# Layer 1's transposes and hub loads within the mixing, and two terms of the convolution's first two pairs ahead of it

## The chip, the cores and the metric

The kernel runs on one core of one Trainium2 chip. The metric is the device time of one launch in microseconds (us). All times below come from the runs and the one profiled execution of the kernel before.

## The reference

Four graph layers act on x of shape (8, 2048, 64): 8 batches, 2048 nodes, 64 features. Each layer is `x = x + gnn(relu(layernorm(x)))`. The adjacency `adj` is 2048 x 2048, zeros and ones with a full diagonal. The first nodes (the hubs) have many neighbours and the last few.

The change lies between the end of layer 0 and the first part of layer 1. Layer 0 ends with a mixing, a softmax of two scores, `tanh(f @ fcW + fcb) @ av`, over two candidates. Layer 1 is a Chebyshev convolution with weights of its own for each node, made from a 16-wide embedding:

```python
w = einsum('nd,dkio->nkio', embedding, weight)          # k = 0, 1, 2
b = embedding @ bias
A_stack = [I, A, 2*A@A - I]
x_g = einsum('knm,bmc->bnkc', A_stack, h)               # h = relu(layernorm(x))
out = einsum('bnki,nkio->bno', x_g, w) + b
```

So it needs A h (the first product in the sense of the layer; the kernel's text and this document call the run that makes it the second product, after layer 0's own adjacency product), and A (A h), made chunk by chunk beside the convolution.

## The kernel before, in words

Data lie either "by feature", as four pairs q of two batches (128 rows of features by 2048 nodes), or "by node", as 16 tiles t of 128 nodes by 512 (8 batches of 64 features). A chunk is 512 nodes, so four tiles. Six large buffers, q0 to q5, are reused through the layers. The program is written in an order, and a planner reorders it for each engine by its own durations, inside the buffers that each tile has. Within an engine's queue the instructions then run in the planned order.

**Mixing** (`mix`, L686 to L773). It steps over four chunks and four pairs. `attend` (L711) scores the next pair ahead; then come the tanh, the mix, the store of x (L767), and the norm of the chunk (`norm_parts`, L271), whose last step, `write` (L697), puts h into `xe` and `xo` (q0 to q3). `each` (L861) brings in and transposes gathered rows. `beside` is `Lists.fill` (L2472): 60 indirect DMAs on POOL read listed blocks of the adjacency, and DVE masks them into `cells`, in bf16. The last chunk's x and its scratch lie in q4 and q5 (`end`, L693), the others' in q6 to q8.

**Passage and second product** (`layer1_near`, L1624). `lists.load` (L2506) loads the adjacency rows of the three hubs (`dense`) and the first columns of the other 13 tiles (`zero`), and DVE casts them to bf16. A loop over 16 tiles transposes h to nodes (L1647), copies it to `ah` in q4 and q5 and stores it in DRAM (`sent[0]`, L1649). Then for each target tile t `Feed.target` (L2629) adds up A h in PSUM: three hub tiles (`dense`, L2610) and LISTED[t] listed pieces (`listed`, L2616). For each piece POOL gathers 128 rows of `sent` (L2578), ACT makes the high part (L2595), DVE the low part (L2596), PE multiplies both with weights that ACT casts from `cells` (L2554) or `dense` (L2564). `finish` (L2634) puts the sum into `ah`; it is stored in `sent[1]` (L1672), and `turn` (L1653) transposes it back into the other halves of `xe` and `xo`. Target 0 has no lists: it reads the 13 tiles from `ah` itself.

**Convolution** (`convolution_near`, L1679). It loads its weights, subtracts (L1697) and doubles (L1698) them, loads the embedding of the first chunk (`load_emb`) and makes A (A h) for that chunk (`product(0)`). Then for chunks 1, 0, 2, 3 in this order, four pairs, eight blocks b and two halves it runs

```python
self.mm(pk, w01[half][:, c], src(q)[:, s], stop=False)      # L1822: terms k = 0 and 1
self.mm(pks[b, half], w2[h, c], aah[h, q], start=False)     # L1829: term k = 2
y = (pks[b, half] + bias) * emb[:, b]                       # L1834, DVE
acc = acc + y                                               # L1840, POOL; the last b on DVE
```

with the next chunk's product spread between the blocks by `advance`. Each f32 matmul shows as two PE passes in the trace.

Of the kernel before, what the change touches and what calls it, by code (L numbers as in the profile page):

```python
# [7 lines left out]
F = mybir.dt.float32  # L8
# [5 lines left out]
OP = mybir.AluOpType  # L14
# [32 lines left out]
F16 = mybir.dt.float16  # L47

# [86 lines left out]
class Kernel:  # L135
# [550 lines left out]
    def mix(self, slots, ind, g, fcw, av, each=None, beside=None):  # L686
# [17 lines left out]
        with (  # L704
# [6 lines left out]
            def attend(ch, q):  # L711
# [9 lines left out]
                if q == 0:  # L721
                    bufs[ch] = end if ch == NC - 1 else [b[:, ch % 2] for b in big]
                    nc.sync.dma_start(bufs[ch][0], self.xs[0][ch])
# [14 lines left out]
            for ch in range(NC):  # L738
                s = slice(ch * CW, (ch + 1) * CW)
                x, sq, xr = bufs[ch]  # L740
                for q in range(NP):
# [22 lines left out]
                    if q < 2:  # L764
                        next(norm, None)
                    next(beside, None)
# [3 lines left out]
            for _ in norm:  # L770
                pass
            for _ in beside:
                pass  # L773
# [8 lines left out]
    def layer0_pairs(self, slots, far):  # L782
# [8 lines left out]
        with tc.tile_pool(reuse_waits="tile", name="k0", bufs=1) as k:  # L791
# [84 lines left out]
            )  # L876
            with tc.tile_pool(reuse_waits="tile", name="filling", bufs=1) as w:
                self.mix(slots, ind, h_t, fcw, av, each, lambda bank: self.lists.fill(cells, w))
# [745 lines left out]
    def layer1_near(self, slots, k2, far):  # L1624
# [11 lines left out]
        with (  # L1636
            tc.tile_pool(reuse_waits="tile", name="cheb", bufs=2) as w,
            tc.tile_pool(reuse_waits="tile", name="cheb_ps", bufs=2, space=PSUM) as ps,
        ):
            lists.load(w)  # L1640
            hub = Hub(w, "first_hub")
            for t in range(NT):
                s = slice(t * P, (t + 1) * P)
                for i, (src, h) in enumerate(((xo, hi), (xe, lo))):
                    pt = ps.tile([P, NP, D], F, name="pt", tag=("acc", "pz")[i], bufs=3)
                    for q in range(NP):
                        nc.tensor.transpose(pt[:, q], src(q)[h, s], ident[h, h])  # L1647
                    self.copy(columns(ah(t), i), pt)
                nc.sync.dma_start(self.sent[0][s], ah(t))  # L1649
                if t < HUBS:  # L1650
                    hub.fill(self, t, ah(t))

            def turn(t):  # L1653
                s = slice(t * P, (t + 1) * P)
                pz = ps.tile([P, NP, P], F, name="pz", bufs=3)
                for q in range(NP):
                    nc.tensor.transpose(pz[:, q], ah(t)[:, q * P : (q + 1) * P], ident)
                for i in range(2):
                    qs = slice(2 * i, 2 * i + 2)
                    nc.scalar.copy(xo.tiles[i][lo, :, s], pz[lo, qs])  # L1660
                    nc.vector.tensor_copy(xe.tiles[i][hi, :, s], pz[hi, qs])

            feed = Feed(self, lists, w, self.sent[0], lambda jt: ah(jt))
            for t in range(NT):
                acc = ps.tile([P, CW], F, name="acc", bufs=3)
                feed.target(acc, t, hub)
                if t < HUBS:
                    nc.scalar.copy(ah(t), acc)
                    lists.hub.fill(self, t, ah(t))
                else:  # L1670
                    feed.finish(ah(t), ah(t), acc, t)
                nc.sync.dma_start(self.sent[1][t * P : (t + 1) * P], ah(t))  # L1672
                if t > 0:
                    turn(t - 1)
            turn(NT - 1)
        with tc.tile_pool(reuse_waits="tile", name="k1", bufs=1) as k:
            self.convolution_near(slots, k)

    def convolution_near(self, slots, k):  # L1679
# [3 lines left out]
        lo, hi = slice(0, D), slice(D, P)  # L1683

        DO = DE * D
        w01 = []
# [1443 lines left out]
```

## Time and profile before

| | us |
|---|---|
| median of 3 runs (lowest to highest) | 2026.12 (2022.63 to 2032.97) |
| profiled execution, its own time | 1975.97 |
| its span, first to last instruction | 1974.2 |
| mixing, first tanh to last mix | 486.8 to 601.7 |
| norm of the last chunk, to its last write | to 617.3 |
| first store of sent[0] issued | 620.0 |
| first indirect gather of the second product | 640.5 |
| first store of sent[1] issued, last | 645.8, 737.8 |
| first chunk's product, first gathered piece at ACT | 747.5 |
| convolution's first result on DVE | 787.5 |

Over the whole span PE was busy 86%, DVE 71%, POOL 52% and ACT 41%. Busy times are of one execution. PE's are modelled: matmuls overlap, so a busy PE is not at its peak. "PEclk" is the share of full speed that was granted to TensorE. In a group's row "128x512 f32" is partitions by elements, "xN" the number of instructions, then come the busy time and the mean of one in ns; behind the second bar is the time that the engine was idle just before these instructions, with what ended it. In a timeline's row the first number is the start, the second the duration of the merged group.

### The profile page before, as it was taken

The page shows a single profiled execution, that of the slowest core. Times are in us where ns is not written, and L with a number is a line of the kernel's source. Part 1 is how long each engine was busy: PE and PEld are TensorE (multiplying, and loading weights), DVE is VectorE, ACT ScalarE, POOL GpSimd, SP SyncE. Part 2 cuts the span into 40 slices and gives each one's busy share as a digit, 9 for nine tenths or more (in the row PEclk, how much of TensorE's full clock was granted, in tenths as well). Part 3 has the DMA queues.
Part 4 walks back from the last instruction along what each step waited for, and adds up shares of the span by engine and source line. Part 5 has one row for each costly group of instructions (what it writes and reads, how often), then busy time and mean ns, then how long its engine had stood idle before and what let it go on. Part 6 is the DMA issues. An engine that isn't in the chain of part 4 may idle for free. (4 is left out here: it accounts for less than half of the span.)

```text
span 1974.2 us, 22337 instructions
## 1 busy us (share of the span) xinstructions
PE 1699.7 (86%) x7066; PEld 971.8 (49%) x7066; DVE 1408.2 (71%) x2389; ACT 809.4 (41%) x1627; POOL 1035.1 (52%) x959
## 2 busy tenths in 40 slices
PE   6859889999997887999999999778989899579885
PEld 2515666665324454444443444356767566345432
DVE  6778778884677674877677656588989676459774
ACT  5712344454664663222111010255666664267300
POOL 1100166766870743876765635266375641478771
PEclk8868899998996888999999989889989999689887
DMA  9740223345335776233131111277788774666665
GB/s 345 263 120 1 77 75 102 109 128 178 99 101 174 239 218 188 78 87 117 47 99 53 48 67 41 96 223 234 246 257 286 222 259 164 228 186 172 183 177 195
DMA packets 124057, 305.20 MB, mean 155 GB/s; under 512 B 29312, under 2 KB 31120, under 8 KB 118160
## 3 DMA queue, kind: packets, MB, share of 16 engines
q0 software_dynamic: 45328, 149.60, 25.2%
q1 hardware_dynamic: 76288, 149.80, 22.5%
q10 hardware_dynamic: 2304, 4.20, 0.6%
q8 instruction: 59, 0.97, 0.2%
q14 instruction: 78, 0.64, 0.1%
HBM read 240.40 MB, written 63.14 MB: 154 GB/s over the span
## 5 line engine op out<-in xcount | busy, mean ns | idle before, releaser
L2578 POOL DMA_INDIRECT raw<-sent,index x300 | 313.8, 1046 | 308.3 <-DVE part_lo L2596 156.3
L2596 DVE TENSOR_TENSOR part_lo<-raw,part_hi 128x512 fp32r<-128x512 f32 x352 | 266.2, 777 | 119.3 <-ACT part_hi L2595 108.8
L2595 ACT CAST part_hi<-raw 128x512 fp32r<-128x512 f32 x352 | 212.5, 619 | 319.0 <-PE acc L176 211.6
L1840 POOL TENSOR_TENSOR half<-half,y 128x512 f32<-128x512 f32 x192 | 247.3, 1318 | 134.0 <-DVE y L1834 128.8
L176 PE MATMUL pk<-q,w 128*128 128x512 f32 (+1 forms) x768 | 301.6, 610 | 2.4 <-DVE q L1724 0.9
L176 PE MATMUL acc<-q,ident 128*128 128x512 f32 x416 | 202.3, 613 | 22.7 <-DVE q L2909 16.5
L176 PE MATMUL acc<-part_hi,weights 128*128 128x512 f32 x365 | 177.0, 488 | 27.3 <-ACT part_hi L2595 26.7
L1834 DVE SCALAR_TENSOR_TENSOR y<-pk,bias,q 128x512 f32<-128x512 f32 x224 | 158.0, 742 | 52.1 <-PE pk L176 32.9
L176 PEld LDWEIGHTS pk<-q,w 128*128 128x128 f32 (+1 forms) x768 | 115.8, 190 | 156.0 <-issue 120.2
L176 PE MATMUL acc<-part_lo,weights 128*128 128x512 f32 x365 | 167.5, 460 | 23.3 <-DVE part_lo L2596 22.7
L2819 POOL DMA_INDIRECT ring<-f_rows,near x121 | 142.8, 1180 | 64.6 <-issue 29.6
L176 PEld LDWEIGHTS acc<-q,ident 128*128 128x128 f32 x416 | 77.1, 194 | 96.4 <-issue 43.6
L2305 POOL TENSOR_TENSOR q<-q,beta 128x512 f32<-128x512 f32 x57 | 76.1, 1337 | 72.4 <-DVE beta L2281 33.8
L176 PEld LDWEIGHTS acc<-part_hi,weights 128*128 128x128 f32 x365 | 73.7, 202 | 79.4 <-ACT part_hi L2595 45.8
L176 PEld LDWEIGHTS acc<-part_lo,weights 128*128 128x128 f32 x365 | 73.9, 202 | 73.5 <-DVE part_lo L2596 57.8
L176 PE MATMUL pp<-adj,x_ind_hi 128*128 128x512 f32 x256 | 89.3, 464 | 0.5 <-DVE q L846 0.3
L2564 ACT CAST hub_weights<-dense 128x384 fp32r<-128x384 bf16 x80 | 40.6, 511 | 102.6 <-PE acc L176 98.2
L2890 DVE TENSOR_TENSOR q<-ring,e 128x1024 f32<-128x1024 f32 x58 | 70.0, 1218 | 8.7 <-PE acc L176 8.5
L2305 POOL TENSOR_TENSOR q<-q,coef 128x512 f32<-128x512 f32 x57 | 63.1, 1108 | 20.9 <-DVE q L2328 17.6
L176 PE MATMUL pp<-adj,x_ind_lo 128*128 128x512 f32 x256 | 72.7, 403 | 0.0
L287 DVE RECIPROCAL std<-std 128x512 f32<-128x512 f32 x16 | 53.6, 3351 | 25.5 <-ACT std L286 21.6
L2489 POOL DMA_INDIRECT listed_raw<-in_adjT_dram,cell x60 | 62.2, 1037 | 16.5 <-issue 15.9
(503 smaller groups left out, 3421.6 us busy)
## 6 DMA issues: line engine op xcount, KB each, us to landing
rows<-in_adj_dram SPq DMA_DIRECT2D x16, 1024.0 KB, 9.2
adj_t<-in_adjT_dram SPq DMA_DIRECT2D x64, 256.0 KB, 3.0
own<-sent SPq DMA_DIRECT2D x52, 256.0 KB, 4.3
raw<-sent SPq DMA_DIRECT2D x52, 256.0 KB, 3.5
sent<-u SPq DMA_DIRECT2D x48, 256.0 KB, 3.7
q<-x SPq DMA_DIRECT2D x10, 1024.0 KB, 5.1
x<-q SPq DMA_DIRECT2D x9, 1024.0 KB, 4.0
links<-squares POOLq DMA_DIRECT2D x16, 512.0 KB, 8.2
```

The lines of the kernel that those rows point to most:

```text
L176: self.nc.tensor.matmul(out, lhsT, rhs, start=start, stop=stop)
L287: nc.vector.reciprocal(std, std)
L1834: nc.vector.scalar_tensor_tensor(y, pks[b, half], bias[:, b : b + 1], emb[:, b], op0=OP.add, op1=OP.mult,)
L1840: add.tensor_add(acc, acc, y)
L2305: self.nc.gpsimd.tensor_tensor(x, x, by.unsqueeze(2).to_broadcast([P, NB, D]), op=OP.mult)
L2489: self.kern.behind(nc.gpsimd.indirect_dma_start(raw[:, i], None, rows, bass.IndirectOffsetOnAxis(ap=self.cell[:, c + i : c + i + 1], axis= ...
L2564: self.nc.scalar.copy(to, self.lists.dense[:, :, i * P : (i + 1) * P])
L2578: self.nc.gpsimd.indirect_dma_start(raw, None, self.rows[:], bass.IndirectOffsetOnAxis(ap=self.lists.index[:, c : c + 1], axis=0),)
L2595: nc.scalar.copy(hi, raw)
L2596: nc.vector.tensor_sub(lo, raw, hi.bitcast(F))
L2819: self.nc.gpsimd.indirect_dma_start(to, None, self.kern.f_rows[:], bass.IndirectOffsetOnAxis(ap=index, axis=0))
L2890: nc.vector.tensor_tensor(y.rearrange("n i (b f) -> n i b f", b=NB), block[:, i : i + 2, : NB * D].rearrange("n i (b f) -> n i b f", b=NB) ...
```

## The change

- *Transposes.* `mix` takes a function `turned`. It does the transposes, copies and the store in `sent[0]` for one tile. Tiles 0 to 11 are done in the last two steps of the next chunk, tiles 12 to 15 after the last norm. The last chunk's x and scratch move from q4 and q5 to the shared buffers, since `ah` now fills q4 and q5.
- *Hub loads.* `fill` also loads `dense` and `zero` in blocks of 128 x 512, and ACT casts them; `load` is gone. `cells`, `dense` and `zero` are u8 instead of bf16.
- *Two terms early.* A class `Conv` holds the convolution's weights, PSUM banks and embedding from the start of layer 1. From target 9 on, `first_part` makes for the first chunk's pairs 0 and 1 the terms k = 0 and 1 (32 matmuls), adds the bias, multiplies by the embedding and sums over b. In the convolution those pairs then have only the term k = 2; its product with the embedding is added to the sum already there, and of its 32 adds half are on DVE.
- *PSUM.* The second product now shares the convolution's banks: 6 for `pk`, which its transposes use too, and 2 for `acc` instead of 3.

```diff
@@ mix @@
                 if q == 0:
-                    bufs[ch] = end if ch == NC - 1 else [b[:, ch % 2] for b in big]
+                    last = ch == NC - 1 and turned is None
+                    bufs[ch] = end if last else [b[:, ch % 2] for b in big]
...
                     if q < 2:
                         next(norm, None)
+                    elif ch > 0 and turned is not None:
+                        for i in range(2):
+                            turned((ch - 1) * TC + 2 * (q - 2) + i, bank)
                     next(beside, None)
...
+            if turned is not None:
+                for t in range(NT - TC, NT):
+                    turned(t, bank)
@@ layer0_pairs @@
+            def turned(t, bank):
+                s = slice(t * P, (t + 1) * P)
+                for i, (src, h) in enumerate(((xo, slice(D, P)), (xe, slice(0, D)))):
+                    pt = bank()[:, : NP * D].rearrange("n (q f) -> n q f", q=NP)
+                    for q in range(NP):
+                        nc.tensor.transpose(pt[:, q], src(q)[h, s], self.ident[h, h])
+                    self.copy(columns(ah(t), i), pt)
+                nc.sync.dma_start(self.sent[0][s], ah(t))
@@ layer1_near @@
-            lists.load(w)
-            hub = Hub(w, "first_hub")
-            for t in range(NT):
...
-                    self.copy(columns(ah(t), i), pt)
-                nc.sync.dma_start(self.sent[0][s], ah(t))
+            conv = Conv(self, slots, k, ps)
+            with tc.tile_pool(reuse_waits="tile", name="cheb", bufs=2) as w:
+                hub = Hub(w, "first_hub")
+                for t in range(HUBS):
+                    hub.fill(self, t, ah(t))
...
+                    acc = ps.tile([P, CW], F, name="acc", bufs=2)
...
+                    if t == NT // 2:
+                        conv.begin()
+                    if t > NT // 2:
+                        for _ in range(2):
+                            next(conv.early, None)
+                turn(NT - 1)
+                for _ in range(8):
+                    next(conv.early)
@@ convolution_near @@
             for _ in product(0):
+                next(conv.early, None)
+            for _ in conv.early:
                 pass
...
+                    begun = place == 0 and q < conv.EARLY
...
-                                self.mm(pk, w01[half][:, c], src(q)[:, s], stop=False)
+                                if not begun:
+                                    self.mm(pk, w01[half][:, c], src(q)[:, s], stop=False)
...
-                                self.mm(pks[b, half], w2[h, c], aah[h, q], start=False)
+                                self.mm(pks[b, half], w2[h, c], aah[h, q], start=begun)
...
+                                if begun:
+                                    nc.vector.tensor_mul(y, pks[b, half], emb[:, b])
...
+                                    own = b == NBLK - 1 or begun and b % 2
+                                    add = nc.vector if own else nc.gpsimd
@@ Lists.fill @@
-        self.cells = pool.tile([P, PLACE[NT], P], BF, name="cells")
+        self.cells = pool.tile([P, PLACE[NT], P], U8, name="cells")
+        self.dense = pool.tile([P, HUBS, N], U8, name="dense")
+        self.zero = pool.tile([P, FAR, P], U8, name="zero")
...
+        def take():
+            if blocks:
+                to, src = blocks.pop(0)
+                raw = w.tile([P, CW], F, name="block_raw", bufs=3)
...
+                nc.sync.dma_start(raw, src)
+                taken.append((to, raw))
+        def store():
+            to, raw = taken.pop(0)
+            self.kern.behind(nc.scalar.copy(to, raw))
...
+            if len(taken) > 1:
+                store()
+            take()
             yield
@@ Conv.first_part @@
+        for q in range(self.EARLY):
+            for b in range(NBLK):
+                for half, src in enumerate(self.xs):
+                    pk = self.bank()
+                    self.kern.mm(pk, self.w01[half][:, b * P : (b + 1) * P], src(q)[:, s])
+                    acc = self.accs[q][half]
+                    y = self.k.tile([P, CW], F, name="early_y", bufs=2) if b else acc
+                    nc.vector.scalar_tensor_tensor(
+                        y, pk, self.bias[:, b : b + 1], self.emb[:, b], op0=OP.add, op1=OP.mult,
+                    )
+                    if b:
+                        add = nc.vector if b % 2 else nc.gpsimd
+                        add.tensor_add(acc, acc, y)
+                    yield
```

## The prediction

> **What bounds the kernel now.** I read the stretches first, busy time by engine, cut where layer 0's mixing ends and where the parts of layer 1 begin: mixing, the passage to layer 1, the second product in two halves, the first chunk's product, the convolution's first chunk.
>
> ```profile
> core 0: us, PE busy (x) PEld busy (x) DVE busy (x) ACT busy (x) POOL busy (x), PEclk, DMA share, GB/s
> 485.00:612.00 127.00, 113.95 (x396) 37.25 (x395) 80.42 (x105) 75.90 (x104) 89.07 (x85) 0.92 0.38 117
> 612.00:634.00 22.00, 13.52 (x131) 11.40 (x132) 19.48 (x34) 10.73 (x27) 0.00 (x0) 0.50 0.61 199
> 634.00:690.00 56.00, 46.62 (x153) 28.83 (x154) 35.59 (x57) 36.70 (x75) 36.49 (x36) 0.87 0.77 241
> 690.00:742.00 52.00, 42.14 (x162) 30.22 (x160) 36.55 (x63) 32.15 (x72) 26.19 (x27) 0.83 0.73 220
> 742.00:787.00 45.00, 32.30 (x96) 18.39 (x98) 18.36 (x28) 16.89 (x35) 15.78 (x15) 0.80 0.64 193
> 787.00:903.00 116.00, 113.72 (x372) 51.48 (x369) 92.67 (x108) 28.40 (x58) 88.80 (x72) 1.00 0.31 88
> ```
>
> In the passage POOL does nothing and PE runs at half clock. In both products no engine is full: they wait on chains. The convolution's first chunk is PE's (98%), with DVE at 80% behind it. Next the timelines of the passage, engine by engine (start, duration, what ended the idle time):
>
> ```profile
> 611.64 5.67 DVE L701 TENSOR_TENSOR q<-q,bank 64x512 f32<-64x512 f32 x8 [2.16 <-PE bank L176]
> ...
> 617.45 4.10 PE L1647 MATMUL pt<-ident,q 64*128 64x64 f32 x56 [2.22 <-DVE q L701]
> ...
> 631.95 1.23 DVE L2512 CAST dense<-dense_raw 128x2048 bf16<-128x2048 f32 x1 [0.88 <-DMA dense_raw<-in_adjT_dram]
> ...
> 626.23 9.61 SPq L1649 DMA_DIRECT2D sent<-q  x12
> ...
> 640.46 1.33 POOL L2578 DMA_INDIRECT raw<-sent,index  x1 [44.59 <-DMA sent<-q]
> ```
>
> All transposes wait for the last write of the norm (617.3). The first gather needs all sixteen stores of sent, the last issued at 635.8; it starts 4.6 us later. The third hub load holds PE's first product matmul until 633.8. Last, the groups by shape, from the second product (634 to 742) and then from the convolution's first chunk (787 to 903):
>
> ```profile
> L2596 DVE TENSOR_TENSOR part_lo<-raw,part_hi 128x512 fp32r<-128x512 f32 x60 | 40.4, 692 | 16.7 <-ACT part_hi L2595 14.1 <-ACT hub_weights L2564 1.8
> L2595 ACT CAST part_hi<-raw 128x512 fp32r<-128x512 f32 x60 | 36.8, 619 | 28.6 <-DMA raw<-sent,index 23.8 <-PE acc L176 2.8 <-DVE part_lo L2596 1.7
> ...
> L1840 POOL TENSOR_TENSOR half<-half,y 128x512 f32<-128x512 f32 x48 | 64.2, 1368 | 18.4 <-DVE y L1834 18.2
> L1834 DVE SCALAR_TENSOR_TENSOR y<-pk,bias,q 128x512 f32<-128x512 f32 x56 | 39.2, 740 | 7.9 <-POOL half L1840 4.3 <-PE pk L176 3.3
> L2596 DVE TENSOR_TENSOR part_lo<-raw,part_hi 128x512 fp32r<-128x512 f32 x31 | 38.1, 1249 | 9.6 <-ACT part_hi L2595 9.4
> ```
>
> The second product waits for gathers (ACT 23.8 us for DMA) and hands the wait on to DVE and PE. The same subtraction takes 0.69 us there and 1.25 us where POOL adds beside it. DVE's own eight adds in the first chunk took 9.72 us, 1.2 each.
>
> **What the Trainium skill says.** "SBUF — State Buffer", section "Who interferes with whom": a DVE instruction with two SBUF inputs contends with a GpSimd one that reads SBUF, through one shared read interface. The trace agrees: 692 against 1249 ns. "TensorE: Matmul & The Clock Gate", section "What's actually happening": the clock is gated to half after an idle window of about 3.4 us. It agrees: after 604.7 to 609.5 without matmuls the clock is 0.50, and passes start 0.43 us apart instead of 0.23. "ScalarE: Activation LUTs", section "What ACT_TABLE_LOAD costs": one element per cycle and lane, fp32 and bf16 alike. Here 512 f32 took 0.62 us and 384 bf16 0.51; no run shows u8.
>
> **The change part by part** (us; minus is saved).
>
> *Mixing.* Twelve tiles' transposes come in: 96 at 0.073 (56 in 4.10) is 7 of PE; 24 copies, half on ACT at 0.38, half on DVE at 0.42, are 4.5 and 5. The hub blocks are 16 ACT casts to u8; by the nearest row (0.62) 9.9. ACT goes from 76 to 90 of 127, DVE from 80 to 85. SP gets 16 loads and 12 stores, 0.33 each or 9, between its x loads and stores; the DMA share was 0.38, and 7 MB in 127 us add 55 GB/s to 117. Each SP store waits for its copy, and what queues behind it is the next block load, three buffers ahead of its cast. POOL gets nothing, but the last chunk's x now shares chunk 1's buffer: chunk 1's norm ended at 564.0, a load of this size took about 5 to land, and POOL's add on it stood at 569.1, with gathers queued behind: 0 to 2. No engine fills; but the stage is a chain of 16 steps of 7.4, and a foreign ACT instruction in front of a tanh costs up to its 0.6. If a quarter of the 14 us on ACT lies on the chain, that is **+4** (0 to +12; no gain, since nothing leaves).
>
> *Passage.* After 617.3 only 32 transposes (2.3) and eight copies over three banks remain: about 3. The last store is issued at 620.5, the first gather starts 4.6 later, at 625.1 instead of 640.5: 15.4 earlier. Target 0's 32 matmuls took from 633.8 to about 645 beside the gather's latency; they can begin by 620, since the hub cells are there and most tiles were made earlier, and end near 631. The first gathered piece reached ACT at 644.7 and will at 630 or 631. The six weight loads, 1.5 MB, and 3.1 of DVE preparation move here; SP was idle from 607.2 to 618.6, so they should land before the last stores. **-14** (-16 to -11; late weight loads would put DVE behind them).
>
> *Second product.* Early units are 32 (2 pairs, 8 blocks, 2 halves), and the generator is called 14 times beside targets 9 to 15, 8 times after the last turn, 10 times in the first chunk's product. All together they are 64 PE passes at 0.43, 27.5; on DVE 32 times 0.742 is 23.7, and 16 adds at 0.69 to 1.22 are 11 to 19, I take 15; on POOL 12 adds at 1.37 are 16. Idle now: DVE 15.4 in 690 to 742 and 26.6 in 742 to 787, 42 against 39. The hole from the last product store (737.8) to the first gathered piece (747.5) is the best cover: nothing but preparation runs, and 8 units want 9 of DVE. In 690 to 742 the 14 units bring 17 to DVE's 36.6 of 52: 53. Warm PE helps there, but queued behind a POOL add that waits for y are the next gathers. acc also falls from three banks to two. If a third of those 17 is on the path: **+5** (0 to +15).
>
> *First chunk's product.* The weight loads no longer meet its first gather, which took 7.0 to reach ACT (740.5 to 747.5) where the median landing is 4.4: 2. The clock was 0.80 and would be held up by early passes: 1. The ten units' 12 of DVE find 26.6 idle. **-3** (-6 to +2).
>
> *Convolution's first chunk*, 787.5 to 903.2. PE loses 64 passes, but 12 of those ran ahead (755.9 to 763.3), so 52 times 0.43, 22. DVE takes over: for the two begun pairs 32 products at 0.68 (what L1724 takes from PSUM) are 21.8 and 16 adds at 1.2 are 19.4; the other two keep 32 at 0.74, 23.7, and 4 adds, 4.9; the next chunk's 31 subtractions at 1.1 (POOL adds 40 times instead of 48) are 34. Sum 104, at 95% use 110 against 116: **-6** (-12 to 0). PE's gain is cut to a quarter because DVE is late next.
>
> *u8 cells.* 209 ACT casts read u8 instead of bf16 (0.49 and 0.51 each). By the skill's rate the estimate is no difference; a tenth more would be 10 on an engine that is busy 41%: **0** (-1 to +3).
>
> Sum: +4 - 14 + 5 - 3 - 6 + 0 = **-14**. The profiled execution took 1975.97 (span 1974.2 and 1.8 around it) and would take 1962. It lies 2.5% below the median of the runs, 2026.12; I carry the difference over: **2012**.
>
> **The rivals.** *Slower: DVE becomes the bound from target 9 to the end of the first chunk.* Now it is busy 147.6 of these 213 us. Added are 39 early and about 12 in the chunk, and each of the 12 early POOL adds holds a DVE subtraction for up to 1.37: 16. That is 215 in 213; at 93% use 231, +18. With mixing at +8 and the passage at -14 it ends at +12, **2038**. It decides from the point where this region grows by more than 10. For it: part_lo's 1249 ns, and queues in order. Against: 26.6 idle in the first chunk's product, and the adds are split so that neither engine has them all.
>
> *Given back.* The passage gains 14, mixing takes 8, the second product 10, the first chunk's product and the convolution give 3 each: -1, **2025**. It is also what comes if the planner, which orders instructions by its own durations, puts the early units where they delay gathers. For it: the ACT chain in the mixing. Against: no engine is above 75% there but PE.
>
> *More.* Warm PE in the products (0.23 instead of 0.43) and a mixing that hides all: 0 - 15 + 0 - 5 - 10 = -30, **1996**. Against it, the waits in the second product are for DMA, which a warm PE doesn't shorten.
>
> **How the numbers follow.** Forecast 0.52, slower 0.21, given back 0.18, more 0.09. 0.5% (10 us) is about what a measurement of this kernel can tell from no change. The forecast's own range is 2003 to 2021; a fifth of it lies within 0.5%, and of given back a tenth lies beyond it on either side: faster 0.52, same 0.25, slower 0.23. The range leaves out one in ten on each side: 1996 to 2040; its upper end is the slower rival's.
>
> **What would show it.** Right: the first indirect gather of sent about 15 us earlier than 640.5, less what mixing grows, and 7 to 9 after the norm's last write instead of 23; no DVE cast of dense in the passage; a mixing of 127 to 133 from its first tanh; the first gather of the first chunk's product landing in under 6; early products on DVE before 787; a first chunk of about 110 with DVE above 93% and PE below it. Wrong: mixing longer by 10 with ACT waited for; part_lo above 0.9 us in the second product with POOL waiting for y; a second product longer by 10; a first chunk as long as before, which would say that the early terms were only moved. Faster by 30 would mean that the clock, not the gathers, held the products.

## The result, and the profile after

The changed kernel takes **2020.29 us** (median of 17 runs, 2011.1 to 2028.18); the kernel before took 2025.41 beside it (17 runs, 2008.44 to 2032.97). The ratio is 0.9981, 95% interval 0.9961 to 1.0001: no change that this measurement can tell. A second comparison, in another set, gave 0.9989 (0.9969 to 1.0010). The forecast was 2012, faster by more than noise.

The profiled execution took 2018.47 us (span 2016.6). The stretches of the changed kernel, cut as those of before (mixing, passage, second product in two halves, first chunk's product, the convolution's first chunk):

```profile
core 0: us, PE busy (x) PEld busy (x) DVE busy (x) ACT busy (x) POOL busy (x), PEclk, DMA share, GB/s
486.00:632.00 146.00, 130.81 (x504) 44.81 (x504) 96.08 (x125) 86.98 (x133) 88.61 (x85) 0.91 0.44 141
632.00:638.00 6.00, 5.48 (x32) 4.71 (x32) 4.34 (x10) 6.00 (x14) 0.00 (x0) 0.50 0.51 182
638.00:694.00 56.00, 45.17 (x152) 27.52 (x151) 38.78 (x61) 37.53 (x79) 37.25 (x36) 0.88 0.81 230
694.00:750.00 56.00, 47.99 (x178) 29.48 (x176) 49.98 (x77) 30.12 (x67) 31.73 (x29) 0.97 0.63 189
750.00:799.00 49.00, 42.42 (x130) 23.52 (x132) 39.96 (x60) 19.41 (x38) 27.79 (x24) 0.86 0.54 167
799.00:911.00 112.00, 102.77 (x316) 44.19 (x313) 96.40 (x121) 28.84 (x58) 75.80 (x64) 0.94 0.31 89
```

The passage has nearly gone. The first chunk's product is as long as before, but DVE is now busy 40 of 49 us in it, where it had 20 of 50. In the convolution's first chunk DVE is at 86% and PE has lost 56 passes, yet the stretch is only 4 us shorter.

The timeline of the passage in the changed kernel (start, duration, what ended the idle time):

```profile
626.03 5.67 DVE L702 TENSOR_TENSOR q<-mix,bank 64x512 f32<-64x512 f32 x8 [2.07 <-PE bank L177]
...
631.76 2.81 PE L893 MATMUL bank<-ident,q 64*128 64x64 f32 x25 [0.36 <-DVE q L702]
...
632.71 2.78 SPq L895 DMA_DIRECT2D sent<-q  x4
...
638.02 1.13 POOL L2583 DMA_INDIRECT raw<-sent,index  x1 [18.28 <-DMA w1v<-in_W1T_dram]
```

Only the last chunk's transposes and four stores follow the norm's last write; the first gather comes 6.3 us after it, where it came 23.1 after. The groups by shape of the second product (638 to 750), answering to those of before:

```profile
L2601 DVE TENSOR_TENSOR part_lo<-raw,part_hi 128x512 fp32r<-128x512 f32 x60 | 43.0, 744 | 12.0 <-PE acc L177 3.7 <-ACT part_hi L2600 3.5 <-remote 2.8
...
L2721 DVE SCALAR_TENSOR_TENSOR early_y<-pk,bias,q 128x512 f32<-128x512 f32 x10 | 7.4, 750 | 0.3
```

and of the convolution's first chunk (799 to 911):

```profile
L2601 DVE TENSOR_TENSOR part_lo<-raw,part_hi 128x512 fp32r<-128x512 f32 x31 | 32.0, 1048 | 5.8 <-ACT part_hi L2600 5.7
...
L1827 POOL TENSOR_TENSOR early<-early,y 128x512 f32<-128x512 f32 x16 | 21.1, 1336 | 24.6 <-DVE y L1818 24.5
L1818 DVE TENSOR_TENSOR y<-pk,q 128x512 f32<-128x512 f32 x32 | 20.7, 681 | 8.2 <-PE pk L177 4.3 <-POOL early L1827 3.8
```

In the begun pairs POOL waits 24.5 us for the products on DVE. A product costs 681 ns where the fused one cost 740, and the 16 adds that DVE now makes itself are 17.4 us more.

All runs came in four sets, each beside runs of the kernel before; at least the last three were on three different chips. The medians of before were 2025.4, 2033.7, 1983.0 and 1978.2; only ratios within a set are compared. The profiles differ mainly in layers 2 and 3. In the stages around the change two executions of one kernel agree within 1.3 us (before) and 3 us (changed). Two kernels with the same instructions in the same order up to the convolution (both moves without early terms, and both moves with the first terms left out, on different chips) differ by 3.5 us in the mixing and 4.6 in the second product. So the stages are compared across sets, but a difference of less than 5 us between sets is not read as an effect. They are, in us: mixing (first tanh to the norm's last write), passage (to the first gather of `sent`), second product (to the last store in `sent[1]`), first chunk's product (to the convolution's first result on DVE) and first chunk (to the moment when SyncE turns to its store of x; the store itself follows 9.7 us later in every run).

| kernel | mixing | passage | second product | first chunk's product | first chunk | sum | ratio to before (95%) |
|---|---|---|---|---|---|---|---|
| before, two executions | 130.6, 130.2 | 23.1, 22.7 | 97.3, 98.6 | 49.7, 49.5 | 115.6, 115.6 | 416.4, 416.5 | 1 |
| changed, two executions | 143.6, 143.6 | 6.3, 6.3 | 112.0, 109.0 | 48.8, 49.3 | 112.1, 112.0 | 422.8, 420.3 | 0.9981, 0.9989 |
| both moves, no early terms | 146.3 | 6.3 | 104.4 | 36.6 | 115.5 | 409.2 | 0.9935 (0.9908 to 0.9962) |
| hub loads moved | 139.7 | 19.2 | 97.9 | 39.8 | 115.6 | 412.1 | 0.9957 (0.9936 to 0.9977) |
| hub loads moved, early terms | 139.1 | 19.3 | 110.1 | 49.4 | 115.5 | 433.4 | 0.9996 (0.9972 to 1.0020) |
| early opening only | 130.4 | 27.3 | 94.7 | 38.6 | 117.2 | 408.1 | 0.9927 (0.9903 to 0.9950) |
| transposes moved | 139.2 | 6.3 | 133.5 | 38.0 | 117.2 | 434.2 | 1.0100 (1.0062 to 1.0138) |
| both moves, casts on DVE | 139.3 | 6.5 | 99.6 | 38.3 | 117.2 | 400.9 | 0.9909 (0.9875 to 0.9942) |
| the same, early terms | 137.2 | 6.6 | 109.0 | 48.7 | 115.4 | 416.8 | 0.9967 (0.9952 to 0.9981) |
| the same, early terms thin on DVE and POOL | 139.4 | 6.4 | 101.4 | 43.2 | 112.9 | 403.3 | one run |
| hub loads moved, casts on DVE | 129.1 | 19.2 | 94.4 | 37.8 | 117.1 | 397.7 | 0.9936 (0.9915 to 0.9956) |
| both moves, first terms left out (casts on ACT) | 142.8 | 6.3 | 99.8 | 38.5 | 119.3 | 406.7 | one run |

Every kernel but the first opens the convolution's weights and banks before the second product, as the change does, and has u8 cells. With the banks comes a point that bears on what follows: in the kernel before the convolution's own product had one bank for its sums (`acc`), in all the others it has two, shared with `side`.

### The profile page after: what moved, and what is told of

It reads as the page before. It is cut to its first block, busy times and chain, and to the rows that moved or that the text cites. A ratio compares the mean times of both kernels' runs of the same rounds, so it can differ in the third digit from the quotient of the medians.

```text
span 2016.6 us, 22406 instructions
## 1 busy us (share of the span) xinstructions
PE 1725.1 (86%) x7066; PEld 974.3 (48%) x7066; DVE 1450.3 (72%) x2445; ACT 818.0 (41%) x1643; POOL 1036.1 (51%) x963
## 5 line engine op out<-in xcount | busy, mean ns | idle before, releaser
L177 PE MATMUL pk<-q,w 128*128 128x512 f32 (+1 forms) x768 | 309.8, 617 | 2.0 <-DVE q L1716 0.9
L1827 POOL TENSOR_TENSOR half<-half,y 128x512 f32<-128x512 f32 x168 | 213.3, 1299 | 116.4 <-DVE y L1820 111.2
L177 PE MATMUL acc<-q,ident 128*128 128x512 f32 x416 | 209.9, 630 | 41.1 <-DVE q L2995 19.4
L177 PE MATMUL acc<-part_lo,weights 128*128 128x512 f32 x365 | 173.1, 475 | 49.4 <-DVE part_lo L2601 45.2
L177 PE MATMUL acc<-part_hi,weights 128*128 128x512 f32 x365 | 172.4, 475 | 23.8 <-ACT part_hi L2600 13.4
L1820 DVE SCALAR_TENSOR_TENSOR y<-pk,bias,q 128x512 f32<-128x512 f32 x196 | 138.4, 744 | 47.3 <-PE pk L177 30.3
L177 PEld LDWEIGHTS acc<-part_lo,weights 128*128 128x128 f32 x365 | 74.2, 203 | 113.6 <-DVE part_lo L2601 83.3
L2569 ACT CAST hub_weights<-dense 128x384 fp32r<-128x384 uint8 x80 | 40.5, 511 | 85.3 <-PE acc L177 84.0
L2500 POOL DMA_INDIRECT listed_raw<-in_adjT_dram,cell x60 | 62.7, 1045 | 16.5 <-issue 15.9
```

Of the source, the lines that this page charges most:

```text
L177: self.nc.tensor.matmul(out, lhsT, rhs, start=start, stop=stop)
L1820: nc.vector.scalar_tensor_tensor(y, pks[b, half], bias[:, b : b + 1], emb[:, b], op0=OP.add, op1=OP.mult,)
L1827: add.tensor_add(acc, acc, y)
L2500: self.kern.behind(nc.gpsimd.indirect_dma_start(raw[:, i], None, rows, bass.IndirectOffsetOnAxis(ap=self.cell[:, c + i : c + i + 1], axis= ...
L2569: self.nc.scalar.copy(to, self.lists.dense[:, :, i * P : (i + 1) * P])
```

## The experiments

The theory from the profile after: the two moves cancel, since mixing gives back what the passage gains, and the early terms lengthen the second product by more than the convolution returns. The rival: the early terms gain what the convolution shows and the rest is a difference between executions.

### The kernel before, a second execution

> The kernel before, unchanged, for a second profiled execution. The one profiled before the prediction was 50 us below its own median, nearly all of it in the gathering stages of layers 2 and 3, so its stages are no fair base for those of the changed kernel. If the early terms truly lengthen the second product by some 10 to 15 us, this execution's first gather to last store of the second product stays at 97 to 100 us although its total is 2015 to 2030; if most of the +14.7 us was a difference between executions, it comes out at 104 or more. Mixing (first tanh to the norm's last write) is expected at 130.5 plus or minus 2 and the passage from there to the first gather at 23 plus or minus 1[...].

2041.41 us in all, 65 more than the first execution, and nothing of it in these stages (416.4 and 416.5): second product 98.6, mixing 130.2. The total is beyond the 2015 to 2030 that was expected. The changed kernel's longer second product is thus no difference between executions, and the profile that the prediction rested on was sound where the change lies.

### Both moves without the early terms

```diff
-    EARLY = 2
+    EARLY = 0
```

> The change without its early terms: transposes and hub loads in the mixing, the convolution's weights and banks opened before the second product, no term begun early. Theory A (the two moves cancel: mixing +13, passage -17): 4 us faster than before, 2016 to 2022, second product 97 to 102. Theory B (the early terms cost the second product 10 us or more and the convolution returns 4): 8 to 10 us faster than the changed kernel, 2010 to 2014. Theory C (the early terms are worth what the convolution shows, -4 to -8, and the longer second product is a difference between executions): 4 to 8 us slower than the changed kernel, about 2025. In the profile: mixing +13, passage 6 to 7 whichever theory holds.

0.9935, against 0.9981 with the early terms (another set; the intervals just touch). The passage is as in the changed kernel, mixing 2.7 longer with the same instructions in the same order. The early terms cost 7.6 us in the second product (4.6 by the second execution) and 12.2 in the first chunk's product and return 3.4: theory B, but with less than its 10 in the second product and most of it in the first chunk's product, where none of the theories had looked. That stage in both kernels, the stretch from the last store to the copy of the chunk's second tile (columns as above), without early terms:

```profile
744.20:768.80 24.60, 18.97 (x69) 10.82 (x69) 10.94 (x19) 11.48 (x24) 13.53 (x14) 1.00 0.69 219
```

and in the changed kernel:

```profile
750.00:784.20 34.20, 30.42 (x85) 16.02 (x85) 32.96 (x48) 11.83 (x24) 25.39 (x22) 0.86 0.48 141
```

DVE is busy 11 us of 25 without the early terms and 33 of 34 with them. Its groups there in the changed kernel:

```profile
L2721 DVE SCALAR_TENSOR_TENSOR early_y<-pk,bias,q 128x512 f32<-128x512 f32 x18 | 13.1, 743 | 0.9 <-POOL early L2726 0.7
L2601 DVE TENSOR_TENSOR part_lo<-raw,part_hi 128x512 fp32r<-128x512 f32 x11 | 10.0, 906 | 0.2 <-ACT part_hi L2600 0.2
L2726 DVE TENSOR_TENSOR early<-early,early_y 128x512 f32<-128x512 f32 x10 | 7.5, 759 | 0.0
```

Of the 32 early results on DVE, 20 stand in these 34 us (18 here and two that begin a sum) and only 12 in the second product. The gathers' own subtraction has gone from 693 to 906 ns beside POOL's early adds, and waits for nothing: up to the second tile the stage is DVE's.

### Only the hub loads moved; and with the early terms

```diff
-   self.mix(..., lambda bank: self.lists.fill(cells, w), turned)
+   self.mix(..., lambda bank: self.lists.fill(cells, w), None)
-   for t in range(HUBS): hub.fill(self, t, ah(t))
+   for t in range(NT):   # transposes, copies, store in sent[0]; hub.fill for the hubs
 # first kernel: EARLY = 0; second: EARLY = 2, as in the change
```

> Only the hub loads in the mixing (with 8-bit cells); the 32 transposed tiles are made after the norm's last write as before, no early terms. Theory A1 (the three shared banks make the transposes dear in the mixing, the hub casts are cheap): mixing +1 to +3 over before, passage 10 to 15 instead of 23, so 6 to 11 us faster than before, and faster than the run with both moves. Theory A2 (the 20 casts on ScalarE are what lengthens the mixing): mixing +8 to +10, passage 10 to 15, so within 3 us of before. In the waits of the mixing, A1 has GpSimd's addition of x waiting for ScalarE's copies no longer than before (3.6 us), A2 still 10 us or more.

> The hub loads in the mixing and the early terms, with the transposes after the norm's last write as before. Beside the run with the hub loads alone it has only the early terms more. Theory B (early terms lose): 5 us or more slower than the hub loads alone. Theory C (they gain): 4 to 8 us faster than the hub loads alone, and if A1 holds too, the fastest of the four, 10 to 15 us below before. Second product 97 to 102 under C, 108 to 114 under B; first chunk of the convolution 112 (105 to 113) under both.

A1 falls: mixing is at +9.5 with the hub loads alone, with no transposes in it (the expectations' "20 casts" are 16 in the trace), and POOL's additions wait 12.2 us for ACT's copies. ACT's groups in this mixing ("issue" is time in which the engine waited for nothing that the profile shows):

```profile
L721 ACT ACTIVATE tanh<-p,cols 128x1024 f32<-128x1024 f32 x32 | 34.7, 1113 | 31.2 <-PE p L177 20.2 <-issue 11.0
...
L2496 ACT CAST dense<-block_raw 128x512 uint8<-128x512 f32 x12 | 7.4, 615 | 0.0
```

The casts are 9.3 us of ACT (12 here and 1.9 for `zero`), and mixing grew by the same. With the early terms the second product is 12.2 longer, the first chunk's product 9.6, and the first chunk no shorter; the five stages together are 21.3 longer, the whole is 9.4 us slower than without (2035.2 against 2025.8). C falls. Where the rest comes back is taken up below, with the changed kernel's second execution.

### Only the early opening; only the transposes

```diff
 # opening only: dense and zero are loaded in the passage and cast on DVE, turned is None, EARLY = 0
+                lists.load(w)
                 hub = Hub(w, "first_hub")
 # transposes: the same, but turned is given to mix
```

> One part alone: the convolution's weights, bias and PSUM banks are opened before the second product; transposes and hub loads stay after the norm's last write, nothing is begun early (cells and hubs are 8 bit as in the change). Theory O (the runs with moves owe their short first chunk's product, 24 instead of 37 us, to the weights alone, which no longer wait in front of it): mixing 130, passage and second product together 121 as before, first chunk's product 24 to 25, so 10 to 13 us faster than before and level with the run with both moves. Rival (the hub loads' move shortens it): 35 to 37 and the time of before. A second rival: the six weight loads now meet the hub loads in the passage, which grows by 3 to 5.

> Transposes in the mixing and the early opening, hub loads in the passage as before, no early terms. From the runs with and without the transposes' move: mixing 137 (130 and 6.6), passage and second product 111 to 117: with the hubs landing some 15 us after the norm's last write as before, 117; if only the gathers mattered, 111. First chunk's product 24 to 25. So 8 to 16 us faster than before. If the transposes' cost in the mixing comes only together with ScalarE's casts (both want ScalarE), mixing 131 to 133 and the run is the fastest so far.

Theory O holds in the whole and in the stage: 0.9927 with nothing moved but the weights and banks, as much as the run with both moves gained, and a first chunk's product of 38.6 (22.7 up to the second tile's copy, where 24 to 25 stood). The five stages account for 8.4 us of it; the kernel before was not profiled in this set, so where the rest lies is open. In the first chunk's product ACT waited as follows (in all, times, longest), in the kernel before, second execution:

```profile
ACT hub_weights L2564 <- PE acc L176: 15.1, 5, 8.6
ACT part_hi L2595 <- DMA raw<-sent,index: 11.6, 5, 7.1
```

and with the early opening:

```profile
ACT part_hi L2612 <- DMA raw<-sent,index: 11.1, 6, 4.3
ACT hub_weights L2581 <- PE acc L177: 3.1, 4, 1.9
```

The wait for gathers hardly changes in sum. The first gathered piece reaches ACT 7.7 us after the last store instead of 9.8, which is 2 of the 11 us. The larger part is a wait for PE. In this stage PE runs twelve passes of the convolution's first terms ahead, and they need the weights. In the kernel before, DVE finishes the weights only some 20 us after the last store, and the twelve passes then stand in one block in front of the second target's hub products (first line); with the early opening the first six run in the wait for the first gather (second line), the others two at a time between the gathered pieces:

```profile
761.69 7.73 PE L176 MATMUL pk<-q,w 128*128 128x512 f32 x12 [0.38 <-issue]
...
742.38 2.82 PE L177 MATMUL pk<-q,w 128*128 128x512 f32 x6
```

The longest wait, 8.6 us, is ACT's behind that block. All the kernels with the early opening and full first terms show the spread passes, and the kernel whose first terms are left out, which has no such passes, takes the same 38.5. No run changed the weights alone, and the second bank for the product's sums may have a part in it: the one bank of the kernel before was free for the second target at 765.4, after DVE had prepared the weights ahead of emptying it, and the hub products began at 768.9, after the block. The rival on the passage has its part too: 27.3 instead of 23, given back as a second product of 94.7.

Transposes without hub loads were a miss, 20 us slower than before where 8 to 16 faster stood. Mixing and passage came as expected. The waits from 630 to 700 and SyncE's queue in that kernel:

```profile
PEld acc L177 <- ACT hub_weights L2573: 35.4, 1, 35.4
...
DVE w L2675 <- DMA w<-in_wk_dram: 12.7, 2, 12.1
```

```profile
637.54 1.86 SPq L2668 DMA_DIRECT2D w<-in_wk_dram  x3
...
642.11 0.63 SPq L2520 DMA_DIRECT2D dense_raw<-in_adjT_dram  x1
...
655.22 6.51 SPq L2520 DMA_DIRECT2D dense_raw<-in_adjT_dram  x2
```

In this order the hub loads stand on SyncE's queue behind the convolution's weights, and on DVE their casts stand behind the weights' subtraction, which waits 12 us for its data. `dense_raw` has one buffer, so the second and third hub load each wait for the cast before (655.2, 661.4); PE waits 35 us for hub weights. The expectation had taken the hubs' landing from the kernel before and left the queue out. With the loads in this order the transposes' move doesn't pay without the hubs' move; another order was not run.

### The hub casts on DVE; the transposes' own cost

```diff
-            self.kern.behind(nc.scalar.copy(to, raw))
+            self.kern.behind(nc.vector.tensor_copy(to, raw))
 # both kernels: EARLY = 0; the second also has turned = None, the transposes in the passage
```

> Both moves and the early opening, no early terms, with the 20 hub casts in the mixing on VectorE instead of ScalarE. Theory A2 (ScalarE's casts stand in front of tanh and square root, which the chain of the mixing waits for): mixing 137 to 140 instead of 146, the rest as in the run with both moves, so 6 to 9 us faster than that. Rival (the loads themselves, on SyncE's queue and beside the gathers, lengthen the mixing): mixing 145 to 147, no difference. A third outcome is that VectorE is as dear as ScalarE, as it takes part in each step of the chain: also 145 or more, but then ScalarE waits less and VectorE is what it waits for.

> Hub loads in the mixing with casts on VectorE, transposes in the passage, early opening, no early terms. Splits the mixing's remaining 9 us of the run with both moves: hub loads with VectorE casts +2 to +4 and transposes +6 (mixing 132 to 134), or the loads themselves +6 to +9 (mixing 136 to 139). Passage and second product 113 to 117, first chunk's product and convolution 155. With 132 to 134 it is 14 to 17 us faster than before, level with the run with both moves (0.991); with 136 to 139, 10 to 12 us.

With the transposes, 139.3, where both moves with casts on ACT took 142.8 to 146.3 in four executions: A2's 137 to 140. Without them it is clearer: 129.1, a little below before, against 139.7 and 139.1. The same loads on SyncE's queue and the same casts cost nothing on DVE and some 10 us on ACT. A2 is shown. A cast is shorter there too (duration: lowest, median, highest), in the kernel without transposes:

```profile
L2496 DVE CAST dense<-block_raw x12: 412/419/549, 508.0 to 598.7; 128x512 uint8<-128x512 f32 x12
```

and its tanh waits for PE alone, with no "issue" behind it:

```profile
L721 ACT ACTIVATE tanh<-p,cols 128x1024 f32<-128x1024 f32 x32 | 34.4, 1112 | 21.0 <-PE p L177 21.0
```

The transposes alone are then 10.2 us of mixing (139.3 less 129.1), where 6 were expected, while passage and second product together gain 7.5 (113.6 to 106.1). Step by step, the time from one mix to the next grows by up to 2.6 us where tiles are transposed, 7.8 in all, and the last norm by 2.6; whether PE's added 11.4 us of busy time, the copies or the three shared banks set that was not separated. The two costs don't add: beside casts on ACT the transposes cost only 3 to 7 (142.8 to 146.3 against 139.1 and 139.7), which stays unexplained.

Both kernels are faster than the kernel before, and their intervals lie below the changed kernel's. Among 0.9909, 0.9936 and 0.9927 (opening alone) the measurement can't choose. What the three share is the opening, and that no term is begun early.

### The first terms left out

```diff
-                                if not begun:
+                                if place > 0 or q > 1:
                                     self.mm(pk, w01[half][:, c], src(q)[:, s], stop=False)
 # EARLY = 0; the term k = 2 then begins the bank; casts on ACT
```

> Both moves, and in the convolution's first chunk the terms k = 0 and 1 of the first two pairs are left out altogether (32 matmuls, 64 passes, 27 us of TensorE), with VectorE and GpSimd doing the same work as before. This is what beginning them early could return at most, had it cost nothing on VectorE. Theory D (VectorE paces the first two pairs, 26.7 and 24.3 us of work in 26.8 and 30.4 us): the first chunk shortens by 2 to 7 us of 127.5. Theory P (TensorE paces it): by 20 us or more, to 100 to 107.

The first chunk took 119.3, with the terms 115.5 (both moves) and 117.2 (both moves, casts on DVE, same set): not shorter at all. P's 20 us did not come, and D's return of 2 to 7 was still too much. The stretch without the terms and, below, with them (casts on DVE):

```profile
773.70:893.00 119.30, 109.65 (x316) 46.94 (x315) 95.20 (x108) 28.61 (x58) 88.67 (x72) 0.86 0.30 84
```

```profile
771.50:888.70 117.20, 114.90 (x368) 52.01 (x367) 91.64 (x108) 28.39 (x58) 89.26 (x72) 0.99 0.31 85
```

52 passes fewer, and PE's busy time falls by 5 us only: the clock sinks to 0.86 and the rest of its passes stretch. Pair by pair it can be seen where. Each entry is the time from the pair's first result on DVE to the next pair's, and how much of it the clock stood at half (us):

| kernel | pair 0 | pair 1 | pair 2 | pair 3 |
|---|---|---|---|---|
| before; both moves | 26.8, 0 | 30.4, 0 | 29.9, 0 | 27.8, 0 |
| both moves, casts on DVE | 26.8, 0 | 30.5, 0.5 | 31.5, 2.9 | 27.9, 0 |
| both moves, first terms left out | 27.0, 18.3 | 34.0, 15.8 | 29.9, 0 | 27.8, 0 |
| changed | 23.8, 6.8 | 28.2, 6.8 | 31.7, 0 | 27.8, 0 |
| hub loads moved, early terms | 23.6, 6.8 | 28.4, 6.8 | 35.0, 6.8 | 27.9, 0 |

Pair 2 keeps its terms in every kernel. PE has no gap in it, and the time at half clock adds about half of itself: 2.9 us add 1.6, and 6.8 add 3.3 (35.0 against 31.7). So there PE sets the pace. This is also the difference between 115.5 and 117.2, and the reason why the hub loads with early terms showed no shorter first chunk. In pairs 0 and 1 the run has 33 and 19 passes fewer, but its clock stood at half for 34 of the 61 us. It shows that the missing passes returned nothing, not what these pairs would take at full clock, and so it doesn't show that DVE and POOL alone pace them. In the changed kernel's pair 0, though, DVE is full, 23.0 of 23.8 us.

### The whole change with casts on DVE; the early terms thin

```diff
+                    n = 1 if b else CW
                     nc.vector.scalar_tensor_tensor(
-                        y, pk, self.bias[:, b : b + 1], self.emb[:, b], op0=OP.add, op1=OP.mult,
+                        y[:, :n], pk[:, :n], self.bias[:, b : b + 1], self.emb[:, b, :n],
+                        op0=OP.add, op1=OP.mult,
                     )
 # and the adds over [:, :n]
```

> The whole change, early terms included, with the hub casts in the mixing on VectorE. Beside the run with both moves and casts on VectorE (ratio 0.991) it has only the early terms more. If these cost what they cost in the first comparison (second product +7.5, first chunk's product and first chunk +8.8), the way from the first tanh to the first chunk's store is 14 to 18 us longer than there (401 to 417), ratio 0.996 to 1.000. If they only cost so much because ScalarE's casts and they met in one plan, 401 to 405 and the ratio stays at 0.991.

> The same with the early terms' 28 results after the first of each sum cut to one column (the sums of those columns alone are formed; the rest of the first two pairs' sums is left out). TensorE's 64 early passes, the banks, the order of the program and the convolution with begun pairs stay. Theory D (VectorE's 48 early instructions are what lengthens the two products): second product back to 100 to 103, last store of the second product to first chunk's store back to 150 to 154, so 14 to 18 us less than the full early terms. Theory P (TensorE's passes, or banks held, lengthen them): 3 us less at most.

The early terms cost 15.9 us here (416.8 against 400.9): 9.4 in the second product, 10.4 in the first chunk's product, less 1.8 and a mixing that came out 2.1 shorter. With the same 64 passes of PE and the same banks, but one column per result on DVE and POOL (the first result of each sum stays whole), the second product is 101.4, as forecast, and the first chunk's product 43.2: 7.6 of the 9.4 and 5.5 of the 10.4 are gone. First chunk's product and first chunk come to 156.1, where 150 to 154 stood. In the first chunk's product, up to the second tile, DVE's groups are

```profile
L2601 DVE TENSOR_TENSOR part_lo<-raw,part_hi 128x512 fp32r<-128x512 f32 x12 | 8.3, 693 | 5.5 <-ACT part_hi L2600 5.5
L2722 DVE SCALAR_TENSOR_TENSOR early_y<-pk,bias,q 128x1 f32<-128x1 f32 x18 | 3.8, 214 | 3.8 <-POOL early L2728 2.5 <-PE pk L177 1.0
```

The subtraction is back at 693 ns and waits for ACT again. Theory D is shown for the larger part: 13.1 of the 19.8 us in the two products are the early terms' work on DVE and POOL. The other 6.7, most of it in the first chunk's product, are left to PE's passes, the banks or the thin instructions themselves. The passes are the likeliest: up to the second tile this run took 28.1 us (22.5 without early terms) and PE was busy in 28.0 of them. That was not separated further, and the run is a single one.

### The changed kernel once more

> The changed kernel once more, beside the kernel before. In its first profile the part up to the convolution's third chunk store was 6 us longer than before, yet its median was 4 us lower (interval from 8 lower to equal). If the stages repeat (mixing 143.6, passage and second product 118.3, first chunk's product and convolution 160.9), the surplus has to come back in the layers after it, about 10 us. Theory R (the order planned for layer 2's first gathers differs in the kernels with early terms, and is the better one): ratio 0.996 to 1.000 again. Theory N (chance): ratio 1.001 to 1.005, as the stages say.

0.9989, so R's side, though N's lower end (1.001) is the interval's upper end. The stages repeated within 3 us. Some of what they lose comes back behind the first chunk, in two places. From the third chunk's store of x to the fourth's the kernels with early terms took 114.9 to 116.6 us in four of five executions, the others 119.6 to 121.4 in eight of nine; the clock makes that difference (see the last section). In layer 2, from layer 1's last store of x to the moment when SyncE turns to the next, the kernels with early terms took 312.4, 314.7 and 313.3 us in the last set, the others of the last two sets 318.5 to 322.7; in the second set 336.8 against 338.4 to 344.9. In the first set it was the other way round: 331.3 in the changed kernel, 319.3 before. On POOL and DVE the order of layer 2's first instructions (over 110 us) is one and the same in all kernels without early terms, and another in all five executions with them. That this order is the cause was not isolated: no kernel had the one without the other.

## Why the prediction was right or wrong

**Passage, -14 predicted, right in its mechanism.** The first gather comes 16.4 to 16.8 us earlier from the norm's last write (6.3 against 22.7 and 23.1), just beyond the range's -16. But the first gathered piece reaches ACT only 11.7 us earlier (15.7 instead of 27.4). The second product then starts with target 0 still to do, which had run beside the passage: it is 5.2 to 6.5 us longer in the kernels with transposes moved (99.6 against 94.4, 104.4 against 97.9). The step counted the earlier gather as the gain in full.

**Mixing, +4 predicted, +13.2 measured, just beyond its bound of +12.** The failed step is "if a quarter of the 14 us on ACT lies on the chain". By themselves the casts lie on it whole: 9.3 us of casts, 9.5 of mixing, and none when DVE makes them. The transposes cost 9 to 10 by themselves, where their 7 of PE was held to be free. Both together came to 13, not to the sum.

**Second product, +5 predicted, +10.4 to +14.7 measured.** Inside its range. 5 to 12 are the early terms (109.0 or 112.0 against 104.4, 110.1 against 97.9), the rest target 0. Part_lo rose from 692 to 744 ns only; the wait for POOL that the slower rival priced is small. What was late is DVE itself: with its early results cut to one column the second product is at 101.4 instead of 109.0.

**First chunk's product, -3 predicted, -0.2 to -0.9 measured: near, for a wrong reason.** It is the sum of two terms of another size, opening -10 to -13 and early terms +10 to +12. Two steps failed. The prediction priced the earlier weights at 2 for the gather, which came, and 1 for the clock. It saw that twelve passes of the convolution run ahead in this stage, but put at nothing that they stood as a block in front of the hub products, where ACT waited 8.2 and 8.6 us behind them in the two executions. The other is "the ten units' 12 of DVE find 26.6 idle". The opening takes 8 to 10 us of this idle time away with those waits: DVE had 29.7 of 49.7 us idle in the whole stage before, and 19 to 21 in the runs with the opening alone. And 20 results of DVE came there, not ten: the planner, not the source's order of calls, placed them. DVE's busy time there rose by 22.5 us (from 17 with the opening alone to 40) and the stage by 10 to 12, so about half was covered.

**Convolution's first chunk, -6 predicted, -3.5 measured.** That DVE is late next was right for pair 0; "The convolution's first chunk is PE's (98%)" holds for pair 2 by the clock and was not shown for pairs 0 and 1, where the passes left out returned nothing. Pairs 0 and 1 became 5.2 us shorter together, and pair 2, with 102 passes instead of 97, 1.8 longer. The Trainium skill, "Perfetto Trace Analysis", section "Identifying the Most-Contended Engine", says that the busy share of matmuls is no good measure of how close a kernel is to its limit, as pipelined instructions look smaller in the trace than they are. The share misled here too, but the other way: with 52 of 368 passes left out PE was still busy 92%, as the passes looked longer at half clock.

**u8 cells, 0 predicted, right**: a cast of 128x384 took 511 ns from bf16 and from u8, one of 128x512 617 and 618.

In sum -14 predicted and +3.8 to +6.4 measured in this region. The time came to 2020, inside the range and nearest to the "given back" rival's account (2025, with mixing +8 and second product +10; its terms add up to -2, not to the -1 that stands there), not the forecast's. The "slower" rival named the right engine, DVE from target 9 on, but priced it at +18; second product to first chunk grew by 7 to 10 in the runs (270.3 and 272.9 against 262.6 and 263.7), at the edge of its point of decision, 10.

## What to carry to other kernels

Before work is placed in idle time, ask which wait makes that time, and whether the same change removes the wait. Ask the same of work that already runs ahead: what does it wait for, and who stands behind it in the queue? On a chain of short steps, price foreign work on the chain's engine whole; the same casts were free on the engine beside it. When a change has several parts, run each alone: here one unnoticed part, opening the weights early, gained as much in the whole (0.9927) as any combination that was run, and the part with the most arithmetic in it lost. Before fewer matmuls are taken for less time, look at the clock: here it fell to half where passes were left out.

## What the runs showed of the hardware

In nine of the fourteen profiled executions the granted clock fell to half for 6.8 or 10.2 us in the midst of layer 1's convolution, each time 17.3 to 19.4 us after the third chunk's store of x, with no gap above 0.11 us between matmuls in the 8 us before it or while it lasted. From that store to the fourth chunk's it was 121.3 to 121.4 us with the longer fall, 119.6 to 119.7 with the shorter, and 114.8 to 116.6 in the five without. The idle rule of the Trainium skill, "TensorE: Matmul & The Clock Gate", section "What's actually happening" (half clock after an idle window of about 3.4 us), doesn't account for it. No kernel is bound to it: the changed kernel had it once (121.4) and once not (114.9). But of the five executions with early terms only that one had it, and of the nine without only one lacked it; why is open. A single profile can be off by 6 us for it.
